# A graph layer on one Trainium2 core: table rows in two float32r halves, sums in sets of four groups

## The chip, the cores and the metric

The kernel runs on one core of a Trainium2 chip. The metric is the device time of one execution in microseconds (us); several executions are timed and the median is given. Engines are named as in the profile: PE is TensorE (matmuls and transposes), PEld its weight loads, DVE is VectorE, ACT is ScalarE, POOL is GpSimd, SP is SyncE, which here only issues DMAs. DMAs are issued by SP, ACT and POOL, each into its own queue. SBUF is the on-chip memory of 128 partitions, PSUM the eight banks (512 float32 columns each) into which PE writes.

## What is computed

Cut to its core, the reference is one layer of a graph network over N = 12500 nodes with D = 256 features and 200000 edges, `src` to `dst`, sorted by `dst`:

```python
h = jnp.maximum(_layernorm(x, axis=-1), 0.0)
agg = jax.ops.segment_sum(h[src], dst, num_segments=N)
z = (1.0 + eps_gin) * h + agg
t = jnp.dot(z, W1) + b1                       # 256 -> 512
t = jax.nn.relu(_batchnorm(t, g1, bt1))
conv_out = jnp.dot(t, W2) + b2                # 512 -> 256
out = jax.nn.relu(_batchnorm(conv_out + h, g2, bt2))
return x + out
```

`_batchnorm` takes mean and variance over all 12500 nodes, so the second layer can't begin before the last node's first layer is done, and the output not before the second layer is done.

## The kernel before

**Tiling.** The edges are cut into 1563 tiles of 128, and the tiles into NG = 131 groups of GT = 12 (the last has three). The nodes are cut into NCH = 25 chunks of CH = 512 (the last has 212). Since `dst` is sorted, the 1536 edges of a group go to some 96 neighbouring nodes; the kernel relies on their lying within 128 nodes from the group's first one, and on group i's first node lying near STEP x i: group i is added to a window of WIDE = 280 node columns that begins at STEP x i - MARGIN, with STEP 96 and MARGIN 76. A general path for edges that don't fit exists in the same program and isn't run here.

**A group's way.** `gather` (L378) issues one indirect DMA on POOL for each tile (L383): 128 rows of 1 KB, picked by `src`, land in a buffer of 12 KB a partition; there are AHEAD + 1 = 5 such buffers, and group i + 4 is issued at step i. `sums` (L404) makes on DVE a one-hot of twelve 128x128 blocks in one instruction (`oh`, L408: which edge goes to which of 128 nodes) and on PE twelve 128x128 by 256-column float32 products that add up in one PSUM bank (`ps`, L418; the profile shows two records for each float32 product). `join` (L423) copies that sum to SBUF on ACT (`zs`, L425) and makes on DVE a 128x280 one-hot that shifts it to its place in the window (`at`, L427). `put` (L432) multiplies the two (`pz`, L437, two products, four records), and `add` (L442) adds the result on DVE into the one or two chunks that the window touches (`zc`, L450). `z_chunk` (L391) loads a chunk's h, transposed, from the DRAM tensor `h_cols` by SP and scales it on ACT (L397); these are the start values of z. When a chunk of z is complete, `first_layer` (L453) makes t in four slices of 128 features: two products of 512 columns (L459, four records), batch-norm statistics on DVE (L463), a copy on ACT (L464), and one DMA of 1 MB on ACT's queue to `t_tab` (L465).

**Where h comes from.** `h_chunk` (L355) takes a chunk of x, normalises it (`settle`, L323: statistics on DVE at L329, the activation on ACT at L340), stores the rows to the DRAM table `h_tab` by ACT's queue (512 KB a chunk), transposes them on PE (L366) and stores the transposed copy to `h_cols` by SP, after copies of PSUM on DVE (L372) and ACT (L370). The first LEAD = 24 groups can't wait for the table: their rows are gathered from x and normalised in the gather buffer itself by `settle` (twelve activations and six statistics a group). From group 24 on the rows come from `h_tab`.

**Order.** The loop at L473 to L494 writes the program in the order h chunks, gather i + 4, join and put of i - 1, sums of i, add of i - 1, first layer. The order in which each engine really runs is found by the framework's scheduler, which may move instructions past each other where the data allow; before, it placed matmuls of other groups and of the first layer in between. After that loop stand the first batch norm (L496), the second layer over 25 chunks (`py`, L527), the second norm (L536), and the output loop (L540 to L559), none of which the change touches.

Of the kernel before, what the change touches and what calls it, by code (L numbers as in the profile page):

```python
# [7 lines left out]
F32 = mybir.dt.float32  # L8
I32 = mybir.dt.int32
AF = mybir.ActivationFunctionType  # L10
# [8 lines left out]
MARGIN = 76  # L19
AHEAD = 4  # L20
LEAD = 24
# [9 lines left out]
def kernel(  # L31
# [233 lines left out]
    def fast():  # L265
# [24 lines left out]
        with ExitStack() as fs:  # L290
# [7 lines left out]

            with ExitStack() as es:
                ln = es.enter_context(tc.tile_pool(name="ln", bufs=2))  # L300
                gat = es.enter_context(tc.tile_pool(name="gat", bufs=AHEAD + 1))
                sel = es.enter_context(tc.tile_pool(name="sel", bufs=2))
                zcp = es.enter_context(tc.tile_pool(name="zc", bufs=4))
                tsp = es.enter_context(tc.tile_pool(name="ts", bufs=2))
                ps_h = es.enter_context(tc.tile_pool(name="ps_h", bufs=1, space=PSUM))
                ps_i = es.enter_context(tc.tile_pool(name="ps_i", bufs=1, space=PSUM))
                ps_s = es.enter_context(tc.tile_pool(name="ps_s", bufs=2, space=PSUM))
                ps_z = es.enter_context(tc.tile_pool(name="ps_z", bufs=1, space=PSUM))
                ps_t = es.enter_context(tc.tile_pool(name="ps_t2", bufs=2, space=PSUM))
# [3 lines left out]
                col = ps_i.tile([P, WIDE], F32, name="col")  # L313
# [30 lines left out]
                xts = {}  # L344

                def x_chunk(g):
                    if g >= NCH:
                        return
                    n = chunks[g][1] * R
                    xts[g] = ln.tile([P, R, D], F32, name="xt", bufs=4)  # L350
                    if n < CH:
                        nc.vector.memset(xts[g], 0.0)
                    carry(nc.sync, xts[g], x, g, store=False)

                def h_chunk(g):  # L355
                    n = chunks[g][1] * R
                    slots = len(parts[g])
                    x_chunk(g + 2)
                    ht = ln.tile([P, R, D], F32, name="ht")
                    settle(xts.pop(g), -(-slots // 2), slots, ht, "c")  # L360
                    carry(nc.scalar, ht, h_tab, g, store=True)
                    hc = ln.tile([P, DC, CH], F32, name="hc")
                    for d in range(DC):
                        ph = ps_h.tile([P, CH], F32, name="pc")
                        for c in range(slots):
                            nc.tensor.transpose(  # L366
                                ph[:, c * P : (c + 1) * P], ht[:, c, d * P : (d + 1) * P], ident
                            )
# [6 lines left out]
                groups = [(t0, min(GT, NTILE - t0)) for t0 in range(0, NTILE, GT)]  # L375
                gathered = {}

                def gather(i):  # L378
                    t0, n = groups[i]
                    ga = gat.tile([P, GT, D], F32, name="gt")  # L380
                    for t in reversed(range(t0, t0 + n)):
                        rows = left if t == full_tiles else P
                        nc.gpsimd.indirect_dma_start(  # L383
                            out=ga[:rows, t - t0, :], out_offset=None, in_=x if i < LEAD else h_tab,
                            in_offset=bass.IndirectOffsetOnAxis(ap=srcT[:rows, t : t + 1], axis=0),
                        )
                    gathered[i] = ga

                zc = {}

                def z_chunk(c):  # L391
                    if c in zc or c >= NCH:
                        return
                    n = chunks[c][1] * R
                    zc[c] = zcp.tile([P, DC, CH], F32, name="zc")
                    nc.sync.dma_start(zc[c][:, :, :n], h_cols[c, :, :, :n])
                    nc.scalar.activation(zc[c][:, :, :n], zc[c][:, :, :n], AF.Copy, scale=gin1)  # L397
# [4 lines left out]
                summed, placed = {}, {}  # L402

                def sums(i):  # L404

                    t0, n = groups[i]
                    oh = sel.tile([P, GT, P], F32, name="oh")
                    nc.vector.tensor_tensor(  # L408
# [402 lines left out]
```

## Time and profile before

| what | us |
|---|---|
| median of 9 executions | 2618.48 (2604.47 to 2644.34) |
| profiled execution, its own time | 2621.99 |
| span of its profile | 2620.2 |
| first gather from the table begins | 490.9 |
| last gather begins | 2321.3 |
| PE busy | 1413.5 (54%) |
| POOL busy | 1479.6 (56%) |
| DVE busy | 716.6 (27%) |
| ACT busy | 459.9 (18%) |

The span is the stretch that the profile covers, the execution's own time lies 1.8 us above it. "Busy" is the sum of an engine's instructions; instructions that only issue DMAs don't count as busy, other than POOL's gathers, which POOL works out itself. No engine is busy for much more than half of the span. The program runs in stages one after another: inputs and indices (to about 45 us), the table with the groups that come from x (to about 490), the groups that come from the table (to 2322), the last sums, the second layer (from 2373) and the output (from 2542). In the profile a line such as `L425 ACT COPY zs<-ps` names the line of the program, the engine, the operation, and the tile written and read; `<-PE ps L418` behind an idle time means that the instruction of that line and engine released it, and "remote" that the profile could not tell who did.

### The profile page before, as it was taken

Reading aid. Unit: us, or ns where it says so; the run is one execution under the profiler, and the core shown is the slowest. Engines: PE = TensorE matmul, PEld = TensorE weight load, DVE = VectorE, ACT = ScalarE, POOL = GpSimd, SP = SyncE. Lnnn points to the kernel's source line nnn. Section 1 sums busy time; section 2 is a strip of 40 time slices with the busy share of each in tenths; the row PEclk is TensorE's granted clock in tenths of the full one; section 3 lists DMA queues with packets and bytes.
Section 4 is the critical chain, followed back from the end, with each engine's and each line's share of the span. In section 5 each row is a group of like instructions: output and inputs, shape, how many; then the busy total and the mean of one; then the engine's idle time right before and its main releaser. Section 6 shows DMA issues by size and latency. Waiting matters only on the chain.

```text
span 2620.2 us, 14777 instructions
## 1 busy us (share of the span) xinstructions
PE 1413.5 (54%) x4873; PEld 1005.4 (38%) x4873; DVE 716.6 (27%) x1060; ACT 459.9 (18%) x871; POOL 1479.6 (56%) x1575
## 2 busy tenths in 40 slices
PE   1245476644553556455455444544564453578995
PEld 1224354433442434334343333433343342453444
DVE  5244464421221212112211211211221121233444
ACT  1344465510000000000000000000000000013434
POOL 4655556666676566666666666666666665620000
PEclk6667687777776777777777776777787776788996
DMA  5454565433343333333333333333333332328728
GB/s 165 156 168 152 185 220 176 131 112 94 114 123 90 101 116 113 96 121 112 114 95 120 113 120 89 120 96 113 120 113 120 94 114 84 99 77 328 274 82 302
DMA packets 150067, 349.41 MB, mean 133 GB/s; under 512 B 28920, under 2 KB 84366, under 8 KB 143838
## 3 DMA queue, kind: packets, MB, share of 16 engines
q0 software_dynamic: 75008, 204.90, 27.1%
q1 hardware_dynamic: 44182, 91.21, 10.0%
q10 hardware_dynamic: 30792, 52.26, 5.3%
q8 instruction: 41, 0.67, 0.1%
q14 instruction: 44, 0.36, 0.0%
HBM read 284.26 MB, written 64.00 MB: 133 GB/s over the span
## 4 chain that ended last, share of the span: by engine, by line
another core or an unknown queue 48%; PE 26%; issue 10%; ACT 6%; DVE 4%; DMA 3%; POOL 1%; SPq 0%; ACTq 0%; POOLq 0%; DVEq 0%
PE ps L418 11%; PE py L527 6%; PE pz L437 4%; PE ph L459 4%; ACT gt L340 3%; DMA out_dram<-ot 1%; ACT zs L425 1%; DMA zc<-h_cols 1%; DVE st L463 1%; DVE oh L408 1%; PE po L551 1%; ACT ht L340 1%; ACT zc L397 1%; ACT ts L464 1%
## 5 line engine op out<-in xcount | busy, mean ns | idle before, releaser
L383 POOL DMA_INDIRECT gt<-h_tab,srcT x1275 | 1205.1, 945 | 626.5 <-issue 373.4
L418 PE MATMUL ps<-gt,oh 128*128 128x256 f32 x3126 | 772.7, 408 | 79.7 <-ACT gt L340 64.4
L418 PEld LDWEIGHTS ps<-gt,oh 128*128 128x128 f32 x3126 | 652.3, 209 | 198.8 <-ACT gt L340 68.5
L437 PE MATMUL pz<-at,zs 128*128 128x280 f32 x524 | 212.7, 542 | 766.7 <-ACT zs L425 624.7
L408 DVE TENSOR_TENSOR oh<-col,dstT 128x1536 f32<-128x1536 f32 x131 | 229.0, 1748 | 1137.5 <-remote 878.0
L437 PEld LDWEIGHTS pz<-at,zs 128*128 128x128 f32 x524 | 122.4, 250 | 830.5 <-ACT zs L425 647.8
L383 POOL DMA_INDIRECT gt<-in_x_dram,srcT x288 | 272.9, 947 | 186.4 <-ACT zs L425 98.0
L459 PE MATMUL ph<-zc,w1s 128*128 128x512 f32 (+1 forms) x400 | 212.2, 681 | 226.7 <-issue 149.4
L425 ACT COPY zs<-ps 128x256 f32<-128x256 f32 x131 | 48.7, 372 | 1605.7 <-remote 1247.0
L459 PEld LDWEIGHTS ph<-zc,w1s 128*128 128x128 f32 x400 | 84.5, 221 | 333.5 <-issue 242.1
L450 DVE TENSOR_TENSOR zc<-pz,zc 128x560 f32<-128x560 f32 (+9 forms) x203 | 100.9, 527 | 349.6 <-remote 173.1
L527 PE MATMUL py<-tT,w2s 128*128 128x512 f32 (+1 forms) x400 | 170.7, 590 | 12.1 <-ACT tT L520 12.1
L340 ACT ACTIVATE gt<-gt,nbg,rsg 128x256 f32<-128x256 f32 x288 | 149.5, 590 | 3.9 <-DVE nbg L338 1.8
L527 PEld LDWEIGHTS py<-tT,w2s 128*128 128x128 f32 x400 | 76.9, 193 | 106.0 <-issue 87.0
L463 DVE BATCH_NORM_STATS2 st<-ph 128x6 f32<-128x512 f32 (+1 forms) x100 | 67.4, 682 | 174.9 <-PE ph L459 55.1
L329 DVE BATCH_NORM_STATS2 stg<-gt 128x6 f32<-128x512 f32 x144 | 91.5, 687 | 34.2 <-DMA gt<-in_x_dram,srcT 28.4
L464 ACT COPY ts<-ph 128x512 f32<-128x512 f32 (+1 forms) x100 | 57.3, 574 | 217.4 <-DVE st L463 170.7
L520 ACT ACTIVATE tT<-ti,of,sc 128x512 f32<-128x512 f32 (+1 forms) x100 | 72.1, 792 | 101.1 <-issue 86.7
L366 PE MATMUL pc<-ident,ht 128*128 128x128 f32 x196 | 38.3, 328 | 62.4 <-issue 18.0
L427 DVE TENSOR_SCALAR at<-col,shift 128x280 f32<-128x280 f32 x131 | 65.5, 500 | 0.3 <-PE pz L437 0.3
L531 DVE TENSOR_TENSOR yT<-py,yT 128x512 f32<-128x512 f32 (+1 forms) x50 | 33.9, 678 | 110.5 <-PE py L527 108.5
L366 PEld LDWEIGHTS pc<-ident,ht 128*128 128x128 f32 x196 | 27.8, 168 | 81.5 <-DVE hc L372 25.9
(74 smaller groups left out, 392.7 us busy)
## 6 DMA issues: line engine op xcount, KB each, us to landing
t_tab<-ts ACTq DMA_DIRECT2D x24, 1024.0 KB
ti<-t_tab SPq DMA_DIRECT2D x24, 1024.0 KB
gt<-h_tab,srcT POOLq DMA_INDIRECT x1275
xt<-in_x_dram SPq DMA_DIRECT2D x24, 512.0 KB
h_tab<-ht ACTq DMA_DIRECT2D x24, 512.0 KB
h_cols<-hc SPq DMA_DIRECT2D x24, 512.0 KB
zc<-h_cols SPq DMA_DIRECT2D x24, 512.0 KB
yT<-h_cols SPq DMA_DIRECT2D x24, 512.0 KB
```

The costliest lines, as they stand in the source:

```text
L329: nc.vector.bn_stats(st[:, c : c + 2, :].rearrange("p c s -> p (c s)"), v[:, c : c + 2, :].rearrange("p c d -> p d c"),)
L340: nc.scalar.activation(to[:, c, :], v[:, c, :], AF.Relu, bias=nb[:, c : c + 1], scale=rs[:, c : c + 1])
L383: nc.gpsimd.indirect_dma_start(out=ga[:rows, t - t0, :], out_offset=None, in_=x if i < LEAD else h_tab, in_offset=bass.IndirectOffsetOnAxi ...
L408: nc.vector.tensor_tensor(oh[:, :n, :], col[:, :P].unsqueeze(1).to_broadcast([P, n, P]), dstT[:, t0 : t0 + n].unsqueeze(2).to_broadcast([P ...
L418: nc.tensor.matmul(ps, lhsT=oh[:rows, j, :], rhs=ga[:rows, j, :], start=(j == 0), stop=(j == n - 1))
L425: nc.scalar.copy(zs, summed.pop(i))
L437: nc.tensor.matmul(pz[:, d, :WIDE], lhsT=zs[:, d * P : (d + 1) * P], rhs=at, start=True, stop=True)
L450: nc.vector.tensor_add(side, pz[:, :, a - lo : b - lo], side)
L459: nc.tensor.matmul(ph[:, :n], lhsT=w1s[:, d, f * P : (f + 1) * P], rhs=zc[c][:, d, :n], start=(d == 0), stop=(d == DC - 1),)
L463: nc.vector.bn_stats(st1[:, f, c, :], ph[:, :n])
L464: nc.scalar.copy(ts[:, f, :n], ph[:, :n])
L527: nc.tensor.matmul(py[:, :n], lhsT=w2s[:, f, d * P : (d + 1) * P], rhs=tT[:, f, :n], start=(f == 0), stop=(f == HC - 1),)
```

## The change

The change rewrites the part of the fast path from the table to the first layer; what stands ahead of it and behind it is kept.

- **The table.** `h_tab` gives way to `h_two`, with 512 columns a node. For each chunk the first 256 hold `hi`, the rows copied by ACT into a float32r tile, and the other 256 `lo`, what that copy lost (DVE, row minus hi). ACT's queue stores both, 1 MB a chunk. A gather from it brings 128 rows of 2 KB.
- **The sums.** From group 18 on (LEAD was 24) a tile's product is one matmul of a float32r one-hot with 512 float32r columns, both halves side by side, into a PSUM bank of its own for each group of a set (`pss`, four banks). `hold` then copies the lo half by ACT and adds the hi half on DVE. The lead groups use float32 as before, in two of the banks.
- **The order.** The scheduler is turned off (`manual_schedule`): each engine runs its instructions in the order in which the program writes them. The lead loop has 18 steps, each with two h chunks in the first 13, one settled group, and one slice of the first layer. Then come sets of four groups: hold, put and add of the four groups of the set before, with slices of the first layer in between, the one-hots of this set, and its sums, each followed by the gather that reuses its buffer, five groups ahead.
- **First layer by slices.** `first_layer` becomes `slice_of` and `take`, with one PSUM bank; each slice is stored by itself (100 DMAs of 256 KB by ACT's queue in place of 25 of 1 MB). `z_chunk` becomes `z_load` and `z_scale`, called at the end of a step.
- **Memory.** The five buffers of the later groups (24 KB a partition each) lie partly on the bytes of the h chunks' tiles (two buffers) and on those of the six lead buffers (three); a buffer waits for the tiles whose bytes it takes.
- **Sizes.** MARGIN 76 to 64, so that WIDE becomes 256 in place of 280; AHEAD 4 to 5; `zs` and `at` in four buffers, `put` in two.

The diff, cut:

```diff
-MARGIN = 76
-AHEAD = 4
-LEAD = 24
+MARGIN = 64
+AHEAD = 5
+SET = 4
+LEAD = 18
...
+                es.enter_context(tc.manual_schedule())
...
+                LOTS = 5
+                lead = es.enter_context(ExitStack())
+                lgp = lead.enter_context(tc.tile_pool(name="lg", bufs=6))
+                pools = []
+                ohs = own.tile([P, SET, GT, P], F32R, name="ohs")
+                pss = psp.tile([P, SET, 2 * D], F32, name="pss")
...
+                def h_chunk(g):
...
+                    hl = lnp.tile([P, R, 2, D], F32R, name="hl")
+                    hi, lo = hl[:, :n, 0, :], hl[:, :n, 1, :]
+                    nc.scalar.copy(hi, ht[:, :n, :])
+                    nc.vector.tensor_tensor(lo, ht[:, :n, :], hi.bitcast(F32), op=OP.subtract)
+                    carry(
+                        nc.scalar, hl.rearrange("p c s d -> p c (s d)").bitcast(F32), h_two, g, store=True,
+                    )
+                    x_chunk(g + 3)
...
                 def gather(i):
+                    if i >= NG:
+                        return
                     t0, n = groups[i]
-                    ga = gat.tile([P, GT, D], F32, name="gt")
+                    if i < LEAD:
+                        gathered[i] = ga = lgp.tile([P, GT, D], F32, name="gx")
+                    else:
+                        k = (i - LEAD) % LOTS
+                        gathered[i] = pools[k >= 2].tile([P, GT, 2 * D], F32R, name=f"gt{k >= 2:d}")
+                        ga = gathered[i].bitcast(F32)
...
+                def bank(i):
+                    return pss[:, i % 2, :D] if i < LEAD else pss[:, i % SET, :]
...
+                        nc.tensor.matmul(
+                            bank(i), lhsT=oh[:rows, j, :], rhs=ga[:rows, j, :], start=(j == 0), stop=(j == n - 1)
+                        )
+
+                def hold(i):
+                    zss[i] = sel.tile([P, D], F32, name="zs", bufs=SET)
+                    if i < LEAD:
+                        nc.scalar.copy(zss[i], bank(i))
+                    else:
+                        nc.scalar.copy(zss[i], bank(i)[:, D:])
+                        nc.vector.tensor_add(zss[i], bank(i)[:, :D], zss[i])
...
+                def take(c, f):
+                    n = chunks[c][1] * R
+                    ph = slices.pop((c, f))
+                    nc.vector.bn_stats(st1[:, f, c, :], ph[:, :n])
+                    ts = tsp.tile([P, CH], F32, name="ts")
+                    nc.scalar.copy(ts[:, :n], ph[:, :n])
+                    nc.scalar.dma_start(t_tab[c, :, f, :n], ts[:, :n])
...
+                for i in range(LEAD):
+                    if made == NCH and not pools:
+                        ln.close()
+                        pools.append(es.enter_context(
+                            tc.tile_pool(name="ga", bufs=2, side="right", reuse_waits="tile")
+                        ))
+                    if i + AHEAD - LEAD < 2:
+                        gather(i + AHEAD)
+                    if i > 1:
+                        add(i - 2)
+                        done["add"] += 1
+                    for c, f in taken:
+                        take(c, f)
+                    if i > 0:
+                        spots(i - 1)
+                        hold(i - 1)
+                    edges(i + 1)
+                    for g in range(made, min(made + TWO, NCH)):
+                        h_chunk(g)
+                    if i + 1 < LEAD:
+                        settle(gathered[i + 1], GT // 2, GT, gathered[i + 1], "g")
+                    sums(i)
+                    for g in range(made, min(made + TWO, NCH)):
+                        turn(g)
+                        made += 1
...
+                lead.close()
+                pools.append(es.enter_context(tc.tile_pool(name="gb", bufs=LOTS - 2, reuse_waits="tile")))
+                for i in range(LEAD + 2, LEAD + LOTS):
+                    gather(i)
...
+                for i0 in range(LEAD, NG + SET, SET):
+                    here = list(range(i0, min(i0 + SET, NG)))
+                    ripe()
+                    some = pick(SET if here else len(done["slices"]))
+                    for i in before:
+                        hold(i)
+                    for k, i in enumerate(before):
+                        put(i)
+                        add(i)
+                        done["add"] += 1
+                        if k == 1 and here:
+                            edges(here[0])
+                        if k:
+                            for c, f in some[k - 1 : k]:
+                                slice_of(c, f)
+                                take(c, f)
+                    for c, f in some[max(len(before) - 1, 0) :]:
+                        slice_of(c, f)
+                        take(c, f)
+                    for i in here[len(before) > 1 or i0 == LEAD :]:
+                        edges(i)
+                    for i in here:
+                        spots(i)
+                    for i in here:
+                        sums(i)
+                        gather(i + LOTS)
+                    if here:
+                        ready(here[-1])
+                    before = here
```

`edges(i)` makes the one-hot of group i (as L408 does), `spots(i)` the shifting one-hot (as L427), `turn` the transposes and copies of a chunk for `h_cols` (in two of the banks of `pss`), `ready` loads and scales the chunks of z that the groups reach, `ripe` lists the slices of the chunks that are complete, and `pick` takes the next ones from that list.

## The prediction

> **What bounds the kernel now.** I read the table by stages first: the rows are the stage in which the feature table is built, the long gather stage, the sums left after the last gather, the second layer and the output. Columns: window, its length, busy time and count of each engine, granted PE clock, DMA share, GB/s.
>
> ```profile
> 45.00:566.00 521.00, 265.74 (x957) 193.98 (x956) 222.50 (x408) 238.96 (x502) 311.34 (x330) 0.71 0.54 168
> 566.00:2322.00 1756.00, 892.22 (x3144) 664.47 (x3143) 351.42 (x439) 101.09 (x195) 1156.20 (x1224) 0.74 0.36 108
> 2322.00:2373.00 51.00, 37.71 (x150) 28.16 (x149) 17.28 (x34) 7.02 (x16) 0.23 (x1) 0.90 0.33 124
> ```
>
> Two thirds of the span is the second row, and there nothing is full: POOL 1156 of 1756 us, PE 892, DMA 0.36. So the next views are POOL's tile and its timeline.
>
> ```profile
> L383 POOL DMA_INDIRECT gt<-h_tab,srcT x1275: 903/946/958, 490.9 to 2321.3; - x183
> ...
>   issue: 373.4, 1219
>   remote: 198.6, 47
>   PE ps L418: 44.6, 6
> ```
>
> A gather takes 946 ns and 0.30 us pass before the next (2321.29 after one that began 1.25 us earlier), so POOL's own floor is 1.25 us, 12 x 1.25 = 15.0 us for a group of twelve tiles. What it does is (2321.3 - 490.9) / 1274 = 1.437 us, 17.24 a group. The excess of 2.24 us is the wait for a free buffer, "remote" and "PE ps". The table of waits says why buffers come late (total us, times, longest):
>
> ```profile
> ACT zs L425 <- remote: 1247.0, 71, 38.7
> DVE oh L408 <- remote: 878.0, 70, 22.7
> PE pz L437 <- ACT zs L425: 624.7, 52, 38.1
> POOL gt L383 <- remote: 198.6, 47, 6.3
> ```
>
> "Remote" is a release that the profile can't place. The PE and ACT timelines place it:
>
> ```profile
> 1096.58 4.48 PE L418 MATMUL ps<-gt,oh 128*128 128x256 f32 x20
> 1100.90 3.60 PE L459 MATMUL ph<-zc,w1s 128*128 128x512 f32 x8
> 1123.83 6.29 PE L459 MATMUL ph<-zc,w1s 128*128 128x512 f32 x8 [19.33 <-ACT ts L464]
> ...
> 1120.85 0.37 ACT L425 COPY zs<-ps 128x256 f32<-128x256 f32 x1 [25.44 <-remote]
> ```
>
> PE's sums ended at 1101.06; ACT copied them at 1120.85, 19.8 us later, and PE stood. After the last gather the same hand-over takes no time:
>
> ```profile
> 2328.50 5.34 PE L418 MATMUL ps<-gt,oh 128*128 128x256 f32 x24
> 2333.01 0.37 ACT L425 COPY zs<-ps 128x256 f32<-128x256 f32 x1 [5.75 <-PE ps L418]
> 2333.68 1.11 PE L437 MATMUL pz<-at,zs 128*128 128x280 f32 x4
> ```
>
> There a group costs PE 6.1 us. So while gathers run, what PE finishes is seen late by the others (why, this trace can't show), PE gets through a group in 17.24 instead of 6, and POOL runs out of buffers. The stage has two floors: POOL's 15.0, and PE's chain of hand-overs, now 17.24.
>
> **The change, part by part.** (a) *Products.* The two records of a 256-column float32 product are 5.34 / 24 = 0.22 us apart, 0.43 a tile, at full clock. The new one has 512 columns of float32r, which no row shows. Bounds: one 256-column record, 0.22; two records of the 512-column product (3.60 us for 8 gives 0.43 each), 0.86. I take 0.33, between one short and one long record, since the change splits the rows to have one pass over both halves. 48 products of a set: 15.6 us (10.4 to 41.5).
>
> (b) *The rest of PE's set.* Four placements of 1.11 us: 4.4. First-layer slices: 100 over 28 sets is 3.6, each four records (1.7 us) and, with one bank, a bn_stats 0.70, a copy 0.58 and hand-overs before the next: about 3 us, 11 us. Hold and add round trips (copy 0.37, add 0.43, add of up to 0.74 for buffers three and four): about 3 us. Sum 34 us a set, against POOL's 60.
>
> (c) *Hand-overs.* Before, a group has three kinds: sums to copy, placement to add, and 0.77 slices to bn_stats: 2.77, or 11 in four groups. In a set the four sums are handed over once, a set later; two placements and the slices remain: 6.5. ACT's lateness is at most 1247 / 131 = 9.5 us a group (some of it is plain waiting for PE), 38 for four; by count 38 x 6.5 / 11 = 22 us. PE's set is thus 34 + 22 = 56 us: under 60, narrowly, so POOL sets the pace. Lateness is uneven, and five buffers (75 us of POOL's work) absorb one bad set and not several. Bounds of the period: 15.0 (all absorbed) and, in this case, 16.0 (nearly half of today's 2.24 left). I take 15.4, near the floor, because the stock exceeds a whole set.
>
> (d) *Rows of 2 KB.* The gathers now bring 256 KB. The queue's transfers took 27.1% of 2620.2 us for 1563 gathers, 0.45 us each; doubled 0.91, under the 1.25 of an issue. POOL issues as many gathers of as many rows as before: zero added. Bounds: zero to a second instruction's 0.95. Cover gone at 1.25 us of transfer, then each further 0.1 us costs 135 us over 1347 gathers.
>
> (e) *Work added elsewhere.* Per chunk of the table a rounded copy on ACT (1.14, the 128x1024 activation) and a subtraction on DVE (1.23, the 128x1024 addition), 1 MB stored in place of 512 KB; per later group one DVE addition of about 0.42 in the hold, 113 of them; 75 more store issues on ACT at 0.4. In the long stage ACT is busy 101 of 1756 us and DVE 351, so there they cost nothing beyond (b); behind the held instructions wait only the next additions, and POOL not at all, as its queue waits for sums alone. The one-hot still takes 1.75, four a set.
>
> (f) *Lead.* Groups from x are 18 in place of 24, so six groups lose 12 activations of 0.49 spacing and six bn_stats of 0.69, 10 us of ACT and DVE a group. But the 25 chunks go two an iteration for 13 iterations. Before, groups 5 to 18 start 116.9 to 387.3, 20.8 us a group with 1.25 chunks each; now two, and ACT's work for 0.75 chunk more (4 activations x 0.49, sqrt 0.29, hi copy 1.14, column copy 0.58, two or three issues x 0.4: some 5 per chunk plus its waits) adds 0 to 4.8: 20.8 to 25.6. The first iteration starts near 62, after the first gathers have landed and been normalised; the first table gather may go when the last chunk is out, after 13 iterations: 332 to 395. I take 375 for POOL's start of group 18 (340 to 400 with the wait for the reused bytes). SP carries h_cols and x three ahead; its queue was not waited for before.
>
> (g) *After the last gather*: 298.0 us today (the last gather ends at 2322.24 of a span of 2620.2). One set and up to eight slices, some 50 us, against today's 51 to the second layer; unchanged.
>
> *Sum*, against the profiled execution's 2621.99 (span 2620.2, so 1.8 around it; the median 2618.48 is 3.5 less): 375 + 112.25 groups x 15.4 (1728.7) + 298 + 1.8 - 3.5 = **2400 us**. With 340 and 15.0: 2320; with 400 and 16.0: 2492.
>
> The row of granted clock, 0.74 in the long stage and 0.98 in the second layer, bears on (a): after the wait of 19.33 us above, eight records of a slice took 6.29 us where 3.60 is usual. The Trainium skill, "TensorE: Matmul & The Clock Gate", section "HAM oscillation — how this bites in real kernels", says that an idle gap of over about 3.4 us drops PE to half clock and that each restart pays about 1.7 us of throttled time. By that rule a set that starts its sums after idling begins cold; three idles a set would be an estimated 5 us, so 61 instead of 56, 1 us above POOL's 60, and over 28 sets the time 28 us more. The sum above leaves it out, since the 9.5 us a group come from the same stage and hold such starts.
>
> **Rivals.** *Late hand-overs keep today's pace*: if what delays PE's signals depends on time and not on how many there are, the period stays 17.24: 375 + 1935.2 + 296.3 = 2606. For it: every kind of hand-over is late alike. Against: four sums share one.
>
> *The set order binds* (the slower side): PE's program is now fixed, so it stands still in each late hand-over where another group's matmuls could follow before. It decides once PE's set takes over 60 us. If each of 6.5 crossings is as late as today's mean of 9.5, or products cost 0.86, the set reaches 34 + 62 = 96 us, or 34 - 15.6 + 41.5 + 22 = 82. Midway between 60 and 96: 78, 19.5 a group, 375 + 2188.9 + 296.3 = 2860. For it: the single slice bank makes PE wait for DVE and ACT three or four times a set. Against: the stage's sums are seldom needed at once.
>
> *Dearer gathers*: 2 KB rows slow the transfers, at 1.45 us a gather 17.4 a group: 2624. For it: DMA 0.36 becomes some 0.8 in that stage with the stores. Against: the 0.91 above.
>
> *The split does nothing* (float32r as dear as float32): the 82 us just priced, part of the second rival.
>
> **Chances.** Forecast (2320 to 2495) 0.62; late hand-overs unchanged 0.13; set order 0.17; dearer gathers 0.08. A measurement can tell 0.5%, 13 us, from no change: below 2605.4 is faster, above 2631.6 slower. The second case lies at the edge (0.06 faster, 0.05 same, 0.02 slower), the third is slower, the fourth slower save 0.01: faster 0.68, same 0.06, slower 0.26. The range reaches up to 2700, a period of 18.1, which takes in the second and fourth cases and the cheap part of the third.
>
> **What would show it.** Right: gathers 1.25 us apart with few waits of POOL, products about 0.33 us apart, the long stage some 1730 us, ACT's long "remote" waits one a set. Wrong: POOL waiting for sums in most sets (set order), gathers spaced over 1.25 without a release (transfers), a first table gather after 400 (lead).

## The result, and the profile after

The changed kernel takes 2841.97 us (median of 20 executions, 2800.49 to 2880.26) against 2621.18 for the kernel before (62 executions): 1.0796 times as long, 95% interval 1.0764 to 1.0828. Here and below a ratio takes only the executions within 1.5% of the fastest of their kernel, so it can differ from the ratio of the medians. The forecast was 2400 us, faster. The profiled execution took 2822.09 us, its span is 2820.2.

The table by stages of the changed kernel, with the same columns as before (lead, sets, last sums):

```profile
45.00:515.00 470.00, 162.23 (x570) 122.87 (x571) 176.44 (x303) 191.06 (x366) 201.22 (x208) 0.63 0.51 169
515.00:2517.00 2002.00, 792.49 (x2248) 498.08 (x2247) 438.82 (x623) 145.16 (x282) 1276.86 (x1347) 0.68 0.66 193
2517.00:2570.00 53.00, 35.52 (x83) 18.54 (x83) 16.69 (x32) 8.19 (x18) 0.00 (x0) 0.79 0.60 212
```

POOL's gathers from the table, and what POOL stood for (total us, times):

```profile
L415 POOL DMA_INDIRECT gt<-h_two,srcT x1347: 907/949/963, 514.7 to 2515.9; - x193
...
  issue: 391.4, 1280
  remote: 156.1, 25
  PE pss L460: 116.5, 9
  ACT zs L467: 51.6, 1
```

The first gather from the table starts at 514.7, where the sum had 375. A gather is no dearer (949 ns against 946), but POOL still waits, 31 times for 269 us after group 22. The table of waits:

```profile
ACT zs L469 <- remote: 759.8, 12, 80.2
...
ACT ts L512 <- DVE st L510: 434.9, 60, 21.8
...
DVE zc L492 <- remote: 232.7, 32, 22.2
...
DVE st L510 <- remote: 184.9, 30, 10.5
```

The long "remote" waits are still there. The timeline of one set, while POOL streams, shows them on the slices (start, duration, engine; in brackets the idle time before):

```profile
1499.02 3.78 PE L499 MATMUL ph<-zc,w1s 128*128 128x512 f32 x4 [5.56 <-issue]
...
1515.14 0.70 DVE L510 BATCH_NORM_STATS2 st<-ph 128x6 f32<-128x512 f32 x1 [9.04 <-remote]
...
1516.52 3.78 PE L499 MATMUL ph<-zc,w1s 128*128 128x512 f32 x4 [12.29 <-issue]
...
1536.85 0.70 DVE L510 BATCH_NORM_STATS2 st<-ph 128x6 f32<-128x512 f32 x1 [10.45 <-remote]
```

A slice that PE ended at 1502.8 is read by DVE at 1515.14, one that ended at 1520.3 at 1536.85: 12 and 17 us late, and with one slice bank the next slice waits for it.

The 422 us between forecast and profiled execution (2822.1 - 2400) lie in three places: 140 in the lead (514.7 - 375), 273 between the first and the last gather from the table (2002.2 in place of 1728.7; 52 of it is one wait of POOL, between groups 19 and 20, for the copy of a lead group's sum), 9 behind it and around the span. Against before, the first gather of group 18 is 127 us later (387.3), the stretch from there to the last gather 67 longer (1934.0 to 2001.2), the rest 5.

### The profile page after: what moved, and what is told of

Read it like the earlier page. It is cut to its first block, busy times and chain, and to the rows that moved or that the text cites. A ratio compares the mean times of both kernels' runs of the same rounds, so it can differ in the third digit from the quotient of the medians.

```text
span 2820.2 us, 12131 instructions
## 1 busy us (share of the span) xinstructions
PE 1207.3 (43%) x3526; PEld 758.3 (27%) x3526; DVE 754.5 (27%) x1134; ACT 454.1 (16%) x818; POOL 1490.4 (53%) x1575
## 5 line engine op out<-in xcount | busy, mean ns | idle before, releaser
L415 POOL DMA_INDIRECT gt<-h_two,srcT x1347 | 1277.2, 948 | 743.6 <-issue 391.4
L460 PE MATMUL pss<-gt,ohs 128*128 128x512 f32 x1347 | 418.9, 458 | 373.5 <-issue 247.0
L460 PEld LDWEIGHTS pss<-gt,ohs 128*128 128x128 f32 x1347 | 292.9, 221 | 489.2 <-issue 379.6
L481 PE MATMUL pz<-at,zs 128*128 128x256 f32 x524 | 179.6, 490 | 401.9 <-DVE zs L470 287.3
L415 POOL DMA_INDIRECT gx<-in_x_dram,srcT x216 | 211.6, 980 | 253.4 <-issue 222.3
L442 DVE TENSOR_TENSOR ohs<-col,dstT 128x1536 fp32r<-128x1536 f32 x131 | 222.9, 1737 | 0.0
L492 DVE TENSOR_TENSOR zc<-pz,zc 128x512 f32<-128x512 f32 (+8 forms) x187 | 93.0, 523 | 411.9 <-remote 232.7
L460 PE MATMUL pss<-gx,ohs 128*128 128x256 f32 x432 | 122.6, 451 | 93.8 <-ACT zs L467 60.1
L460 PEld LDWEIGHTS pss<-gx,ohs 128*128 128x128 f32 x432 | 99.9, 234 | 120.9 <-ACT zs L467 67.8
L354 ACT ACTIVATE gx<-gx,nbg,rsg 128x256 f32<-128x256 f32 x216 | 108.1, 587 | 9.0 <-DVE nbg L352 6.5
```

The source lines that it names most:

```text
L354: nc.scalar.activation(to[:, c, :], v[:, c, :], AF.Relu, bias=nb[:, c : c + 1], scale=rs[:, c : c + 1])
L415: nc.gpsimd.indirect_dma_start(out=ga[:rows, t - t0, :], out_offset=None, in_=x if i < LEAD else h_two, in_offset=bass.IndirectOffsetOnAxi ...
L442: nc.vector.tensor_tensor(ohs[:, i % SET, :n, :], col[:, :P].unsqueeze(1).to_broadcast([P, n, P]), dstT[:, t0 : t0 + n].unsqueeze(2).to_br ...
L460: nc.tensor.matmul(bank(i), lhsT=oh[:rows, j, :], rhs=ga[:rows, j, :], start=(j == 0), stop=(j == n - 1))
L481: nc.tensor.matmul(pz[:, d, :], lhsT=zs[:, d * P : (d + 1) * P], rhs=at, start=True, stop=True)
L492: nc.vector.tensor_add(side, pz[:, :, a - lo : b - lo], side)
```

## The experiments

Kernels sent together ran on one chip, beside the kernel before. Five chips came up, of two kinds. A signal is the semaphore count that an instruction raises when it ends, and for which the engines that need its result wait. On four chips the kernel before takes 2570 to 2645 us, as in the runs above, and PE's signals are late as in the first profiles; these are called late chips. On one it takes 2268 us and no signal is late in the traces taken there; it is called the prompt chip. Times are compared within a chip.

For the following table the trace's record of PE's semaphore was set against the ends of the PE instructions that signal, each record against the last end before it, so the lateness is a lower bound: the share of signals more than 3 us late from group 22 to the last gather, the pace of POOL in that stretch, and its waits of more than 3.2 us.

| kernel | chip | signals > 3 us late | us a group | POOL's waits |
|---|---|---|---|---|
| before | late | 37% of 233 | 17.23 | 41, 221 us |
| changed | late | 42% of 224 | 17.47 | 31, 269 us |
| a_banks | prompt | 0 of 232 | 15.00 | none |
| a_f32 | prompt | 0 of 297 | 15.02 | none |
| a_lead | late | 46% of 234 | 17.76 | 26, 302 us |
| a_both | late | 40% of 177 | 18.18 | 28, 348 us |
| b_lag | late | 27% of 265 | 17.33 | 15, 123 us |
| al_pause3 (1.3 us) | late | 42% of 226 | 17.64 | 16, 166 us |
| al_pause6 (2.6 us) | late | 0 of 152 | 17.63 | none |
| a_pause (5.2 us) | late | 0 of 181 | 20.21 | its own pauses |

Only PE's signals are late. In the same stretch of the changed kernel's trace none of the 98 recorded signals of ACT and the 210 of DVE comes more than 0.02 us after its instruction's end, and the same holds for the kernel before.

### No stream of gathers: a_still, b_still, a_still_l

```diff
-                gathered = {}
+                gathered, kept = {}, {}
...
+                    if 6 <= i < LEAD or i >= LEAD + LOTS:
+                        kept[i] = gathered[i] = kept[i - (6 if i < LEAD else LOTS)]
+                        return
...
+                    kept[i] = gathered[i]
```

> The changed kernel with POOL's gathers left out from group 6 on in the lead and from group 23 on in the sets (later groups read the rows of earlier ones, so the output is not the layer's). Theory (while POOL streams gathers, what PE finishes is signalled some 9 us late, and the fixed order of a set has about six such hand-overs one behind the other): without a stream the signals come at once, and a set takes PE's own chain, 48 products 11.6 + placements 4 + four slices with their statistics and copies 13 + hold and add 3 = 32 us, in place of 71; the stage of 27 sets lasts about 900 us in place of 2002. A lead step falls from 33 to some 25 us. Rival (the fixed order is that long by itself, each hand-over between engines costs 10 us whatever POOL does): sets stay at 60 us or more, the stage at 1600 or more, lead steps at 33.

> The kernel before with POOL's gathers left out after the first five groups of the lead and the first five from the table (later groups read the rows of earlier ones, so the output is not the layer's). Theory: without a stream a group takes 6 to 8 us as in the last groups of the profile of before, so the 102 groups from group 29 on last about 700 us in place of 1760, and the groups of the lead fall from 20.8 to some 15 us. Rival (lateness belongs to the hand-overs themselves): 15 us a group or more, 1500 us.

> The version with gathers left out after group 5 of the lead and after group 22 (later groups read the rows of earlier ones) again, for a late chip. Theory: without the stream PE's signals are prompt there too, a set takes 24 to 30 us, the time is that of the other chip, 1541 within 20. Rival (that chip's PE signals late at all times): 2000 or more.

The first two came to the prompt chip: 1540.99 and 1447.09 us. All 29 sets' sums of a_still lie between 535.7 and 1260.9, 25 us a set, less than the 32 expected; b_still's PE is busy for all of 725 us in the stage, some 7 us a group. But on this chip signals are prompt with the stream too, so these two only size PE's own chains: neither comes near POOL's 60 us a set. The lead missed: a_still's first gather from the table is at 459.0, a step of 32 to 33 us still, without any stream, where 25 were expected. On a late chip a_still_l took 1608.54, 67 more than the other, 48 of it in the lead (first gather from the table at 507), where a difference of up to 20 was expected; its sums run from 598.3 to 1328.9, 731 us against 725. After 640 us, 10 us behind its last gather, none of its signals is over 3 us late. Without the stream the late chip's sets are as quick as the prompt chip's.

### Slices in four banks: a_banks

```diff
-                        if k:
-                            for c, f in some[k - 1 : k]:
-                                slice_of(c, f)
-                                take(c, f)
...
+                    for k in range(0, len(some), SET):
+                        for b, (c, f) in enumerate(some[k : k + SET]):
+                            slice_of(c, f, b)
+                        for c, f in some[k : k + SET]:
+                            take(c, f)
```

> The changed kernel with the up to four slices of a set made back to back in the four banks of pss, after all holds and placements, and their statistics and copies behind them, in place of one bank that each slice waits for. Theory: three serial hand-overs of about 9 us leave a set of 71, which comes to 60 to 62 or POOL's 60; with some lateness left a period of 15.5 to 16.3 a group in place of 17.84, so 170 to 260 us less: 2580 to 2670. Rival (2 KB rows hold the gathers back, DMA share 0.66 against 0.36): no change, 2842 within 30.

On the prompt chip: 2480.30 against 2268.39, ratio 1.0938 (1.0920 to 1.0956). Its waits show whose pace it is:

```profile
ACT zs L469 <- PE pss L460: 1196.8, 29, 56.7
...
PE pss L460 <- DMA gt<-h_two,srcT: 671.7, 83, 11.0
POOL gt L415 <- issue: 390.1, 1281, 0.3
```

PE waits for gathers, POOL for nothing but its own 0.30 us: 15.00 us a group, with rows of 2 KB. There the sum's floor is real, and nothing is lost in the sets. So the 212 us that it is slower must lie elsewhere, most likely in the lead (first gather from the table at 459.2, and a wait of 34.6 us before group 20); that is inferred, as the kernel before has no trace from this chip. What the four banks do can't be told on this chip; the unchanged changed kernel wasn't run on it.

### Without the halves: a_f32, a_f32_l

```diff
-            h_two = dram.tile([N, 2 * D], F32, name="h_two")
+            h_two = dram.tile([N, D], F32, name="h_two")
...
-                    hl = lnp.tile([P, R, 2, D], F32R, name="hl")
...
+                    carry(nc.scalar, ht, h_two, g, store=True)
...
-                        nc.scalar.copy(zss[i], bank(i)[:, D:])
-                        nc.vector.tensor_add(zss[i], bank(i)[:, :D], zss[i])
+                    nc.scalar.copy(zss[i], bank(i))
```

> The changed kernel without the halves: table rows of 1 KB in float32, products of 256 columns in float32 (two records), the hold a plain copy; sets, fixed order, buffers, lead as changed. Theory (the fixed order and its hand-overs set the set): products cost PE 48 x 0.2 = 10 us a set more, transfers half; the period stays at 17.5 to 18.5, the time at 2800 to 2920. Rival (dearer gathers of 2 KB): the period falls to 16 or less, the time below 2650.

> The changed kernel without the halves (table rows of 1 KB, float32 products of 256 columns in two records, plain hold) again, for a chip on which PE's signals come late. Theory: the period stays at 17.5 to 18.5 as in the changed kernel, since sets alternate with POOL's stream in the same way; the lead ends 85 us earlier, so 2740 to 2780 where the changed kernel takes 2842. Rival (2 KB rows lengthen the period): below 2650. On a chip of 2268: 2362 again.

On the prompt chip 2362.31, ratio 1.0417 (1.0399 to 1.0434): the sets stand at POOL's 15.02 as with the halves, and the first gather from the table is at 373.3 in place of 459.2, 86 us earlier, which with a wait before group 20 that is some 30 us shorter is nearly the whole of the 118 us to a_banks. On a late chip it is the slowest of the versions without pauses: 3002.56, ratio 1.1321 (1.1210 to 1.1431), where 2740 to 2780 were expected. There the lead ends 80 us earlier as well (434.8 against 514.7), so in the sets a group takes about 2 us more without the halves. Which part of the halves saves that (products of one record in place of two, or another) no run tells. Rows of 2 KB don't hold the gathers back on either chip.

### The two kernels again, the lo halves moved, both edits: b_again, a_again, a_lead, a_both

```diff
+                    nc.scalar.copy(hl[:, :n, 0, :], ht[:, :n, :])
+                    x_chunk(g + 3)
+
+                def halves(g):
...
                     if i + 1 < LEAD:
                         settle(gathered[i + 1], GT // 2, GT, gathered[i + 1], "g")
+                    for g in range(made, min(made + TWO, NCH)):
+                        halves(g)
                     sums(i)
```

> The kernel before, unchanged, for its trace on the chip of these runs. Theory (two kinds of chips: on one PE's signals come late while gathers stream, on the other at once): where it takes about 2268 us, POOL's gathers stand 1.25 us apart from the first to the last, the last one starts at about 32 + 1562 x 1.25 = 1985, the long remote waits of ACT and DVE are gone, PE waits for gathers. Where it takes about 2620, the picture of the first profile returns. Rival (2268 has another cause, such as a faster gather): gathers under 1.25 us apart.

> The changed kernel, unchanged. Theory: on a chip of 2268 its sets run at POOL's 15.0 us a group, and it loses only in the lead (group 18 from the table starts at about 459 and POOL stands 35 us before group 20): 2475 to 2485, the time of the version with four slice banks, a ratio of 1.09. On a chip of 2620: 2800 to 2880, ratio 1.08. Rival (the slice bank costs on every chip): 2550 or more on a chip of 2268.

> The changed kernel with one part moved: a chunk's lo subtraction on DVE and its store are issued behind the statistics of the second chunk and of the group, in place of ahead of them, where DVE waits 3.2 us for ACT's hi copy and the next statistics stand behind it, twice a step. Theory (a lead step of 33 us is one chain of DVE and ACT waiting for each other): 6 to 7 us a step less, group 18 starts 75 to 90 us earlier than in the changed kernel, the time 70 to 90 less (near 2395 on a chip of 2268). Rival (the 1 MB stores, or ACT's work itself, set the step): no change within 10 us.

> The lead of the run before this one, and the slices of a set in four banks. Theory: on a chip of 2268 nothing beyond the moved lead, within 5 us of it, since there the sets stand at POOL's 15.0 already; on a chip of 2620 another 170 to 260 us less, since three late hand-overs leave each set. Rival: a gain of the four banks on both.

A late chip: before 2605.44, b_again 2597.77 with the picture of the first profile (17.06 us a group), a_again 2842.61, ratio 1.0850 (1.0754 to 1.0946). a_lead took 2750.74, 92 less, ratio 1.0515 (1.0428 to 1.0602); its first gather from the table is at 444.1, against 514.7. This is the chain it loosens, in the changed kernel's timeline of DVE and ACT in the lead:

```profile
342.55 1.04 ACT L375 CAST hl<-ht 128x1024 fp32r<-128x1024 f32 x1
...
343.62 1.24 DVE L376 TENSOR_TENSOR hl<-ht,hl 128x1024 fp32r<-128x1024 f32 x1 [3.22 <-ACT hl L375]
344.78 1.29 DVE L343 BATCH_NORM_STATS2 stc<-xt 128x6 f32<-128x512 f32 x2
...
348.95 1.04 ACT L375 CAST hl<-ht 128x1024 fp32r<-128x1024 f32 x1
350.03 1.22 DVE L376 TENSOR_TENSOR hl<-ht,hl 128x1024 fp32r<-128x1024 f32 x1 [3.22 <-ACT hl L375]
351.17 3.69 DVE L343 BATCH_NORM_STATS2 stg<-gx 128x6 f32<-128x512 f32 x6
```

DVE stands 3.22 us for ACT's copy, twice a step, with the next statistics queued behind the subtraction, and ACT's next activations wait for those. a_both missed: 2805.59, ratio 1.0737 (1.0664 to 1.0811), 55 us slower than a_lead where 170 to 260 less were expected. Fewer hand-overs stand in a row, but the mean lateness over the recorded signals goes from 5.3 to 7.9 us. Lateness isn't a fixed price for each hand-over.

### Pauses in the stream: a_pause, al_pause3, al_pause6, al_even

```diff
                             in_offset=bass.IndirectOffsetOnAxis(ap=srcT[:rows, t : t + 1], axis=0),
                         )
+                    if i >= LEAD:
+                        for _ in range(12):
+                            nc.gpsimd.iota(idle, pattern=[[1, 280]], base=0, channel_multiplier=0)
```

> The changed kernel with POOL kept busy without a gather for 12 x 0.36 = 4.3 us (twelve index ramps) after each group from 18 on, 5 us with the gaps. Theory (PE's signals come through when the stream of gathers pauses): on a late chip the pauses take the place of POOL's waits for buffers, 15 + 5 = 20 us a group, with POOL's waits on PE near nothing and the mean lateness well under 8 us. Rival (lateness doesn't depend on the stream): 17.84 + 5 = 22.8 a group. On a chip where signals are prompt 20 as well.

> The changed kernel with the moved lo halves of a_lead and POOL busy with three index ramps (1.3 us) after each group from 18 on. Theory on a late chip: 16.3 to 17.0 a group in place of 17.8, 90 to 160 us less than a_lead, ratio 0.99 to 1.02. Rival (needs longer pauses): 1.3 us a group on top, ratio 1.10. On a prompt chip 1.3 x 112 = 146 more than the moved halves alone.

> As the run before with six ramps (2.6 us). Theory on a late chip: 17.6 a group with POOL's waits on PE near nothing, ratio 1.04 to 1.06; if three ramps were too short and six are enough, this one is the faster of the two.

> As al_pause3, the three ramps spread, one after every fourth gather (0.4 us each). Theory (what matters is a pause long enough for what is under way to land, 1.5 to 2.4 us): short spread pauses don't help, ratio 1.08 to 1.10. Rival (any drop in the rate of gathers helps, the stream's length doesn't matter): as al_pause3 or better, ratio 1.02 or less.

a_pause, on a late chip: 3100.26 us, 20.21 a group, as 15.0 + 5.2. Of 181 signals none is over 3 us late. Its waits are those of the prompt chip:

```profile
ACT zs L473 <- PE pss L464: 1809.4, 28, 78.2
...
PE pss L464 <- DMA gt<-h_two,srcT: 1316.1, 95, 17.2
POOL gt L416 <- issue: 416.5, 1344, 2.1
```

So with PE's program unchanged, on a chip where b_lag's and a_f32_l's signals are late, a pause after every twelve gathers makes PE's signals prompt. In the same trace, in the lead, where there are no pauses, one is 33 us late. POOL is as busy with the ramps as with gathers, so it is the gathers that make signals late, and not POOL's being busy. On another late chip (before 2617.33) three ramps, 1.3 us, leave 42% of the signals late and gain nothing (2759.77, ratio 1.0568, 1.0498 to 1.0638); six, 2.6 us, make all prompt, with no wait of POOL on PE left in what it stood for,

```profile
L419 POOL DMA_INDIRECT gt<-h_two,srcT x1347: 905/949/963, 443.9 to 2454.3; - x193
...
  issue: 416.3, 1343
  ACT zs L474: 33.4, 2
  ACT gx L354: 12.4, 1
```

and the pace is 15.0 + 2.6 = 17.63: 2749.38, ratio 1.0522 (1.0460 to 1.0584). Three ramps spread over the group (al_even) gave 2742.12, ratio 1.0513 (1.0444 to 1.0581), with 39% late: neither the 1.08 to 1.10 of its theory nor the 1.02 or less of its rival. All three lie within what a_lead showed (1.0515): a pause that is long enough costs what the waits cost. The intervals overlap, so which of the three is best stays open.

### More room for PE, and pauses in the kernel before: b_lag, b_pause, b_pause24, al_pause24

```diff
-                ps_s = es.enter_context(tc.tile_pool(name="ps_s", bufs=2, space=PSUM))
-                ps_z = es.enter_context(tc.tile_pool(name="ps_z", bufs=1, space=PSUM))
+                ps_s = es.enter_context(tc.tile_pool(name="ps_s", bufs=LAG + 1, space=PSUM))
+                ps_z = es.enter_context(tc.tile_pool(name="ps_z", bufs=2, space=PSUM))
...
+                    if i >= LAG:
+                        join(i - LAG)
+                        pz = put(i - LAG)
```

> The kernel before with more room between PE and the others: four banks for sums in place of two, four one-hots in place of two, two banks for placements, a group's copy and placement three groups behind its sums in place of one, six gather buffers (AHEAD 5, LEAD 25), MARGIN 64, col in SBUF. Theory (on a chip where signals are late, POOL's stream and PE's hand-overs alternate: POOL streams until the buffers that the last release freed are full, then stands some 4.5 us until PE's signals come; before, two groups are freed at a time, 15 + 4.5 / 2 = 17.2): with three to four groups freed at a time 15 + 4.5 / 3.5 = 16.3 a group, 100 us less on a chip of 2605 (2480 to 2530); on a chip of 2268, where POOL is the floor, 2268 within 10. Rival (a fixed lateness of some 9 us for each hand-over, whatever the room): no change within 15 on either.

> The kernel before with POOL filling half of the gather buffer with zeros (128x1536, an estimated 1.2 us from 0.20 us for 128x128 and 0.10 for 128x1) ahead of each group's twelve gathers, which overwrite it. Theory (a stream unbroken for more than ten gathers or so delays PE's signals, a pause lets them through): on a late chip the pauses of 1.2 us replace waits of 2.2 us a group, 16.2 to 16.8 a group from the table, 50 to 110 us less than before (ratio 0.96 to 0.98). Rival (a pause must last some 4 us before signals pass): 1.2 us a group on top, ratio 1.04 to 1.06. On a prompt chip 1.2 x 131 = 160 more, ratio 1.07.

> The kernel before with POOL filling a whole gather buffer with zeros (128x3072, 2.7 us by twice the 1.39 of 128x1536) ahead of the gathers of every second group, so one pause of 3 us in 24 gathers. Theory (a pause of 2.6 us lets PE's signals through, one of 1.3 doesn't, and before POOL already stands 4.5 us in 23 gathers): 15 + 1.4 = 16.4 a group if every such pause is enough, 90 us less than before, ratio 0.965; with two hand-overs needed a pause, 17.2 and no change. Rival (the pauses come on top of today's waits): ratio 1.05. On a prompt chip 180 more, ratio 1.08.

> The changed kernel with the moved lo halves and six ramps (2.6 us) after every second group, where al_pause6 has them after each. Theory: 16.3 a group if two pauses in a set are enough for its hand-overs, 150 us less than al_pause6, ratio 0.995 on a late chip; if each serial hand-over of a set needs a pause of its own, six in a set, POOL waits for buffers on top and the period stays at 17.4 to 17.8, ratio 1.05. On a prompt chip 146 more than the moved halves alone.

All four on late chips. b_lag: 2610.42 against 2607.64, ratio 1.0041 (0.9987 to 1.0096), no gain where 100 us were expected. POOL's streams did become longer, 70 gathers on average in place of 23, and its waits fell to 123 us; but the mean gather grew from 0.945 to 1.040 us, over some 1260 gathers 120 us, more than the 98 us of waits that went. The longest took 2.5 us where before none took 1 us:

```profile
L382 POOL DMA_INDIRECT gt<-h_tab,srcT x1263: 902/949/2529, 486.6 to 2309.0; - x181
```

The edits to the kernel before and to a_lead:

```diff
                     ga = gat.tile([P, GT, D], F32, name="gt")
+                    nc.gpsimd.memset(ga[:, : GT // 2, :], 0.0)
```

```diff
                     ga = gat.tile([P, GT, D], F32, name="gt")
+                    if i % 2:
+                        nc.gpsimd.memset(ga, 0.0)
```

b_pause (the first, 1.39 us each) took 2629.12 against 2617.33, ratio 1.0062 (1.0024 to 1.0100); b_pause24 (the second) 2704.99 against 2592.27, ratio 1.0422 (1.0367 to 1.0477); al_pause24, six ramps after every second group, 2733.94, ratio 1.0452 (1.0376 to 1.0528). b_pause met neither of its forecasts (0.96 to 0.98, or 1.04 to 1.06); the other two came near their rivals' 1.05. One pause in 24 gathers is not enough for either order; the cost of al_pause6 can't be halved that way. No version that does the whole layer beat the kernel before on either kind of chip.

## Why the prediction was wrong

**(c), hand-overs: the step that turned the sign.** It took today's 9.5 us of lateness a group, scaled it by the number of hand-overs (11 to 6.5 in four groups), found 56 us a set under POOL's 60, and let POOL run at 15.4. What the runs show in its place: lateness is no price for each hand-over, it is made by POOL's own unbroken stream. POOL streams until the buffers are full, and then stands until a late signal frees one. Of the late signals, 57 of 85 in the kernel before (from its first gather from the table on) and 43 of 93 in the changed one arrive while POOL stands, which is 14% of the stretch in both. In the kernel before, streams of 23 gathers and waits of 4.7 us on average make 17.2 a group; in the changed one streams of 38 and waits of 8.0 make 17.5. The mean lateness is much the same in both (5.5 and 5.6 us), the longest goes from 23 to 64 us. So an order that lets POOL stream longer paid for it in longer waits.

A long stream also holds back PE's own instructions. In the changed kernel, weight loads and products then follow each other 1.40 us apart, though the profile shows nothing that the four products here and their weight loads wait for:

```profile
1396.72 0.59 PE L460 MATMUL pss<-gt,ohs 128*128 128x512 f32 x1 [2.20 <-issue]
1398.12 0.29 PEld L460 LDWEIGHTS pss<-gt,ohs 128*128 128x128 f32 x1 [2.51 <-issue]
...
1399.52 0.59 PE L460 MATMUL pss<-gt,ohs 128*128 128x512 f32 x1 [2.21 <-issue]
...
1402.32 0.59 PE L460 MATMUL pss<-gt,ohs 128*128 128x512 f32 x1 [2.21 <-issue]
...
1405.12 0.59 PE L460 MATMUL pss<-gt,ohs 128*128 128x512 f32 x1 [2.21 <-issue]
...
1419.37 0.95 POOL L415 DMA_INDIRECT gt<-h_two,srcT  x1 [8.80 <-remote]
```

This happens in eleven stretches of the changed kernel, 203 us in all, each begun after 33 to 53 us in which POOL never stood for 1 us. In b_lag, with streams of 70 gathers, it is 31 stretches and 512 us; in the kernel before, a_banks, al_pause6 and a_pause there is none.

Pauses of 2.6 us bring the signals through at the same pace. No order tried here came below 17 us a group on a late chip, and 15.0 is the pace on the prompt chip without any care. The profile held the hint, prompt signals after the last gather, and the prediction read it as "while gathers run" without asking what a faster POOL would do to it. Shown: that the stream causes it (a_still_l, a_pause, al_pause6). Not shown: by what mechanism in the chip, and why one chip is free of it. POOL's issuing and the DMA traffic that it starts were always stopped together, so which of the two it is stays open.

**(f), the lead: 375 in place of 514.7.** ACT's and DVE's added work was summed as if the two ran beside each other. In the order written by hand each waits for the other: a step is 32 to 33 us even without a stream (a_still, prompt chip, group 18 at 459.0). Of the 84 us between 375 and 459, leaving the halves out gives back 86 (a_f32), and on a late chip 80 (a_f32_l), moving the subtraction alone 71 there (a_lead). The other 56 us (459 to 515) come with the late chip, and they are one delay, of the kind that (c) is about. Between the first and the second step the hi copies are 34 us apart in a_still (62 to 96), 82 in a_still_l (62 to 144) and 92 in the changed kernel (62 to 154); the later steps take 32 us in all three. It falls into POOL's first stream, the gathers of the first six groups (to 123.8 in a_still_l) or seven (to 138.9): there PE stands 45.57 us in a_still_l, and 7.54 in a_still, before the next transposes of the first chunk, for DVE's copy of the ones before. In the changed kernel's trace the signals there are up to 44 us late. (e) had the halves' copies at nothing for the long stage, which holds; their cost was in the lead. The wait before group 20, 52 us here and 35 on the prompt chip, was not in the sum at all: it was folded into "the wait for the reused bytes" with 25 us of room.

**(a), (b): sized too high, and it didn't matter.** Where the stream doesn't hold PE back, 48 products took 11.62 us, 0.24 each, where 0.33 was taken (15.6):

```profile
1476.29 11.62 PE L460 MATMUL pss<-gt,ohs 128*128 128x512 f32 x48
```

A set's own chain is 25 us where 34 was taken. That PE's work is smaller may show on late chips: without the halves, with two records for each product, a group takes about 2 us more there.

**(d), (g): right.** Gathers of 2 KB take POOL 949 ns and on the prompt chip keep 1.25 us apart; the stretch after the last gather is 303.3 where 298.0 was taken.

**The rivals.** "Late hand-overs keep today's pace" is what happened in the sets (17.47 for 17.24); its 2606 fell short by the lead and the wait before group 20. "The set order binds" named 2860, close to the result by luck, for a wrong reason: with fewer waits in a row (a_both) the pace got worse, not better, and PE's set without a stream is 25 us. "Dearer gathers" is out.

On the granted clock: slices in the sets took 3.78 us after waits of 5.6 and 12.3 us, at a granted clock of 0.50, where the same four records took 1.88 at 1.00 in a set without such a wait, and the stage's clock fell from 0.74 to 0.68. The Trainium skill, "TensorE: Matmul & The Clock Gate", section "HAM oscillation — how this bites in real kernels", says that PE starts cold, throttled to half, after a gap of over about 3.4 us, for about 1.67 us. The half clock agrees; here it lasted longer, for all of the 3.78 us. It wasn't what set the pace: with prompt signals the pace is POOL's own sum.

## What to carry to other kernels

Where a stream of software-made gathers feeds PE, ask what the stream itself does to PE's signals before taking the stream's own rate as a floor: look whether hand-overs are prompt when it pauses. An edit that lets the stream run longer can give its gain back in longer waits. And when an order is written by hand, cost a step as the chain of waits between engines, not as the busiest engine's sum: one subtraction queued ahead of the next statistics was worth 71 us of the lead here.

## What was not expected of the hardware

- Chips differ: the kernel before takes 2268 us on one and 2570 to 2645 on the others. On the one no PE signal of the versions traced there is over 3 us late while gathers stream; on the others, without pauses, 27 to 46% are, by up to tens of us, while ACT's and DVE's signals stay prompt. Whether that belongs to the chip or to what else ran on it, no run here tells.
- On the late chips a pause of POOL of 2.6 us after twelve gathers is enough for all signals to come, one of 1.3 us is not.
- After more than 33 us of unbroken gathers on a late chip, PE's own instructions fell to one each 1.40 us for stretches of the changed kernel's trace.
- In streams of 70 gathers on a late chip, single gathers took up to 2.5 us on POOL in place of 0.95.
- A 512-column float32r product follows the one before it after 0.24 us (48 in 11.62), about as soon as one of the two records of a 256-column float32 product (0.22).
